# Five of every 120 edge tiles fetched row by row: three by ScalarE, two by SyncE

## The chip, the cores and the metric

The kernel runs on one core of one Trainium2 chip. Time is device microseconds for one execution; lower is better. Five engines work beside one another, each through its own list of instructions in order: TensorE (PE in the profile; its weight loads are PEld), VectorE (DVE), ScalarE (ACT), GpSimd (POOL) and SyncE (SP). POOL, ACT and SP also issue DMA transfers. Engines wait for one another, and for DMA, through semaphores.

## What is computed

A graph layer over 50,000 nodes with 160 features each and 1,650,000 directed edges, sorted by destination. For every edge the source node's row is taken, multiplied by the edge's four attributes, mixed by small weight matrices and summed into the destination; then comes a node-wise product, a ReLU, a residual and a layer norm.

```python
s, v = x[:, :64], x[:, 64:].reshape(n, 32, 3)
ss, vv = s[src], v[src]                    # a gather of 640 bytes for every edge
...
m = concatenate([out0, out1.reshape(-1, 96)], axis=1)
m_agg = segment_sum(m, dst, num_segments=n)
...
x = layernorm(x + x + relu(h))
```

## The kernel before, in words

The kernel sums x[src] times each of four attributes per destination first and applies the weights afterwards, once per node. Edges come in tiles of 128, one edge to a partition. Six tiles make a group, two groups a pair (12 tiles), and ten pairs a segment of 120 tiles. There are 12,522 tiles in 1,044 pairs.

For each pair the work runs so. `gather` (lines 430 to 440) fills one of four `xg` buffers, each of 12 tiles: POOL issues one indirect DMA per tile (line 437), which brings 128 rows of x of 640 bytes each. `spread` (448 to 458) builds on DVE a 0/1 matrix of destinations, `hot` (452), and multiplies it by the attributes, `ha` (455). `group_sums` (475 to 491) multiplies `ha` by the gathered rows on TensorE, two matmul instructions per tile at line 482, into the PSUM tile `ps`. `turn_sums` (493 to 507) transposes `ps` on DVE into `sums` (497) and adds that to a ring of destination sums (506). Each time a block of nodes is complete, `do_block` multiplies its ring columns by the weights (801), and `norm1`, `norm2`, `norm3` finish the rows. `norm2` is one square root on ScalarE (196), placed in ACT's order one pair after the product; `norm3` is on DVE one pair later and waits for it; SyncE sends the result (`do_send`, 899).

The order on SP, PE, DVE and ACT is the order of the Python program (line 979): the loop over pairs at the end writes it out by hand. DVE turns the sums of pair p-1 while PE works on pair p, and then builds `ha` for pair p+1. POOL has its own order: only gathers. It may run ahead until the next `xg` buffer is still being read by PE, which it learns from PE's semaphore.

One tile of 120 is not gathered by POOL. In `list_rows` (376 to 384) DVE clamps its 128 source numbers (`held`, 381) and turns them into byte offsets (`line`, 382). In `rows_by_scalar` (353 to 374) ScalarE loads 32 offsets at a time into registers (365), and then issues one DMA for each row (369, with a register move before it). Each row adds 16 to one of eight semaphores `landed`; Tile's own tracking of these transfers is switched off. The 128 steps are dealt into ACT's order over ten pairs, from the fifth pair of a segment on (lines 1002 to 1009), and the tile is used four pairs after the last (`spots_in`, 351). PE waits in an instruction of its own (481) until 16 x 128 have arrived. The buffers are `xf`, two of them. 102 of the segments have such a set.

SyncE loads the edge data of the next segment (270 and 276), node rows (744, 777), stores the packed edge rows of a table made on the way (718), and sends results (899), all in its written order.

Of the kernel before, what the change touches and what calls it, by code (L numbers as in the profile page):

```python
# [39 lines left out]
F32 = mybir.dt.float32  # L40
I32 = mybir.dt.int32
BF16 = mybir.dt.bfloat16
U8 = mybir.dt.uint8
# [7 lines left out]
P = 128  # L51
# [26 lines left out]
KM = WS - 1  # L78
REST = 15
LEAD = 3  # L80
NF = 1
FB_ = 2
FBEGIN, FWAIT = 4, 4

def plan(n_nodes, n_edges):
# [24 lines left out]
def tile_gnn_resnorm(ctx: ExitStack, tc: tile.TileContext, x, src, dst, attr, W1, W2, W3, W4, W5, Ws, Wv, out, n_edges):  # L110
# [123 lines left out]
    with tc.tile_pool(name="once", bufs=1) as once, tc.tile_pool(name="raw", bufs=2) as rawp, \  # L234
            tc.tile_pool(name="idx", bufs=2) as idxp, tc.tile_pool(name="rows", bufs=4) as rowp, \
            tc.tile_pool(name="hot", bufs=1) as hotp, tc.tile_pool(name="ops", bufs=3) as op, \
            tc.tile_pool(name="sums", bufs=2) as sump, tc.tile_pool(name="ring", bufs=2) as ringp, tc.tile_pool(name="node", bufs=2) as np_, \
            tc.tile_pool(name="ahead", bufs=3) as aheadp, tc.tile_pool(name="outs", bufs=2) as outp, \
            tc.tile_pool(name="psC", bufs=1, space=PSUM) as psC, tc.tile_pool(name="psK", bufs=2, space=PSUM) as psK, \
            tc.tile_pool(name="psP", bufs=1, space=PSUM) as psP, tc.tile_pool(name="psA", bufs=2, space=PSUM) as psA, \  # L240
            tc.tile_pool(name="psM", bufs=2, space=PSUM) as psM, ExitStack() as later_pools:

        spotp, ownp, fetchp, listp, heldp = (
            later_pools.enter_context(tc.tile_pool(name=name, bufs=bufs))
            for name, bufs in (("spot", 3), ("own", 2), ("fetched", FB_), ("list", 2), ("held", 1)))
        extremes = once.tile([P, 2, NSC], F32, name="extremes")
        count_ = once.tile([1, SG], F32, name="count")
        nc.gpsimd.iota(count_, pattern=[[1, SG]], base=0, channel_multiplier=0, allow_small_or_imprecise_dtypes=True)
# [97 lines left out]
                                                        skip_runtime_bounds_check_because="held within bounds")  # L346
            return spot_of.pop(g)

        fetched, fetches, asked, turns = {}, deque(), [], [0]
        landed = [tc.alloc_semaphore(f"landed{i}") for i in range(4 * FB_)]  # L350
        spots_in = [math.ceil((FBEGIN + per * (i + 1) / NF + FWAIT - per) * PG * G) for i in range(NF)]

        def rows_by_scalar(s, i, line, u):

            turn, xf = turns[0], []
            turns[0] += 1
            sem = landed[turn % len(landed)]

            def one(q, e):
                if not q and not e:  # L360
                    xf.append(fetchp.tile([P, D], F32, name="xf"))
                    fetched[s, spots_in[i]] = xf[0], turn
                if not e:
                    r = q * W + u // NK
                    _, asked[:] = nc.values_load_multi_w_load_instructions(
                        line[r:r + 1, i * W:(i + 1) * W], engines=[ET.Activation], min_val=0, max_val=(N - 1) * 4 * D,
                        skip_runtime_bounds_check_because="held within bounds")
                p = q * W + e
                row = nc.scalar.dma_start(xf[0].bitcast(U8)[p:p + 1], xbytes[ds(asked[e], 4 * D)].rearrange("(o f) -> o f", o=1))
                row.then_inc(sem, 16)  # L370
                tc.no_tile_sem_insts.add(row.ins.name)
                tc.add_to_no_dep_group(f"rows{turn}", row.ins)

            fetches.extend(partial(one, q, e) for q in range(P // W) for e in range(W))

        def list_rows(s, u0, ef):

            line = listp.tile([P, NF * W], I32, name="line")
            held = heldp.tile([P, NF, W], F32, name="held")
            for i, at in enumerate(spots_in):  # L380
                nc.vector.tensor_scalar(held[:, i], ef[:, 0, (u0 + at) % NK], 0.0, float(N - 1), op0=ALU.max, op1=ALU.min)
            nc.vector.tensor_scalar(line, held.rearrange("p i e -> p (i e)"), float(4 * D), None, op0=ALU.mult)
            for i, at in enumerate(spots_in):
                rows_by_scalar(s, i, line, u0 + at)

        def place(cast_):

# [42 lines left out]
        def gather(s, placed, u, n):  # L430

            xg = rowp.tile([P, PG * G, D], F32, name="xg")
            rows = [fetched.pop((s, u + j), None) for j in range(n)]
            for j in range(n):
                if rows[j] is None:
                    rows[j] = xg[:, j, :], None
                    nc.gpsimd.indirect_dma_start(  # L437
                        out=xg[:, j, :], out_offset=None, in_=x,
                        in_offset=bass.IndirectOffsetOnAxis(ap=placed[0][:, u + j:u + j + 1], axis=0))
            return rows  # L440
# [34 lines left out]
        def group_sums(p, rows, ha):  # L475

            ps = psA.tile([P, PG, D], F32, name="ps")
            fresh("ps")
            for j, (xr, turn) in enumerate(rows):
                if turn is not None:  # L480
                    nc.tensor.wait_ge(landed[turn % len(landed)], 16 * P * (turn // len(landed) + 1))
                mm = nc.tensor.matmul(ps[:, j // G, :], ha[:, j].rearrange("p k w -> p (k w)"), xr,  # L482
                                      start=j % G == 0, stop=j % G == G - 1)
                if turn is not None:
                    tc.declare_no_dep(mm.ins, group=f"rows{turn}", reason="their own semaphore is waited for")
                    tc.declare_fence(mm.ins, group=f"rows{turn}")
                if j % G == 0:
                    wrote("ps", mm)
                else:
                    written["ps"][-1].append(mm.ins)  # L490
                yield ps
# [485 lines left out]
                after_pair(p + d, f, b)  # L977
        at_last.close()
        later_pools.enter_context(tc.manual_schedule(engines={ET.SP, ET.PE, ET.DVE, ET.Activation}))
        turning, left = None, 0  # L980
        for p, (s, g, ng) in enumerate(pairs):
            if (p + LEAD) % per == 0 and (p + LEAD) // per + 1 < NSC or not p:
                ahead_ = (p + LEAD) // per + 1
                end = reach(ahead_)
                assert end <= 0 or rows_stored[0] == NR or end <= row_start(rows_stored[0])[0][0]
                raws[ahead_] = load(ahead_)
            if p % per == 0 and s + 1 < NSC:
                after_pair(p + 1, do_cast, s + 1)
                after_pair(p + 2, do_place, s + 1)
                if s + 2 == NSC:  # L990
                    after_pair(p + 4, examine_all)
                    after_pair(p + 6, read_flags)
            rows = gather(s, placed[s], (g - s * SG) * G, ng * G)
            for j, ps in enumerate(group_sums(p, rows, has.pop(p))):
                if j == 1 and turning:
                    turn_sums(*turning)
                    turning = None
                if j == 3 and p + 1 < len(pairs):
                    s1, g1, ng1 = pairs[p + 1]
                    has[p + 1] = spread(placed[s1], (g1 - s1 * SG) * G, ng1 * G)  # L1000
                work(1.0)
                if p % per == FBEGIN and not j:
                    assert len(fetches) == (P * NF if 0 < s < NSC - 2 else 0), (p, s, NSC, len(fetches), len(tasks))
                    begun_at, left = p, len(fetches)
                if left:
                    keep = math.floor(P * NF * (1 - (p - begun_at + (j + 1) / (ng * G)) / per))
                    while left > keep:
                        fetches.popleft()()
                        left -= 1
                if packs and p >= START:  # L1010
                    when = p + (j + 1) / (ng * G)
                    todo = math.ceil(len(packs[0]) * min(1, (when - began) / max(1, due[0] - began)))
                    for step in packs[0][done:todo]:
                        if step:
                            step()
                    done = max(done, todo)
                    if done == len(packs[0]):
                        packs.pop(0), due.pop(0)
                        done, began = 0, when
            turning = p, ps  # L1020
            if p == START - 2:
# [12 lines left out]
            hand_over(p)  # L1034
# [162 lines left out]
```

## Time and profile before

| what | us |
|---|---|
| median of the two timed runs | 17926.19 |
| the two runs | 17913.42 and 17938.96 |
| the profiled execution's own time | 18036.58 |
| its span, first to last instruction | 18034.8 |
| POOL busy in the span | 11796.2 |
| DVE busy | 7589.3 |
| PE busy | 7025.2 |
| ACT busy (arithmetic only) | 172.2 |

How to read it: busy time counts work of the engine proper. Register moves and the issuing of DMAs by ACT and SP are not in it, so an ACT that is busy for 1% of the span may still have no time left: its issues stand in the timeline under ACTq, those of SP under SPq. A timeline row gives the start, the time from the first to the end of the last instruction of the row, the engine, the line, the operation, how many are merged, and in brackets the idle time before the first with what ended it. "issue" there means that the profile shows nothing that was waited for; "remote" means a semaphore whose writer the profile could not name.

### The profile page before, as it was taken

To read this page: it belongs to the slowest core of one execution; us is meant where nothing else is said; L and a number is where in the kernel's file an instruction comes from. 1 tells how busy PE (TensorE), PEld (TensorE's weight loads), DVE (VectorE), ACT (ScalarE), POOL (GpSimd) and SP (SyncE) were. 2 spreads that over 40 slices of the span, in tenths; PEclk is the share of its full clock that TensorE was granted. 3 is DMA by queue.
4 is the path that set the end of the run, shared out by engine and by line. 5 is a ranking of instruction groups with operands and counts; after the bars stand their busy time and mean duration, and the time that the engine had idled before them with its cause. 6 is when DMAs were issued, how large, how long until landed. Compare 5 with 4: busy or idle time off the path is not lost.

```text
span 18034.8 us, 122135 instructions
## 1 busy us (share of the span) xinstructions
PE 7025.2 (39%) x28971; PEld 6194.0 (34%) x28972; DVE 7589.3 (42%) x12430; ACT 172.2 (1%) x273; POOL 11796.2 (65%) x12433
## 2 busy tenths in 40 slices
PE   3343343334433333333334334333333433333333
PEld 3233333333333333333333333333333333333333
DVE  7344245334524443453345245434533453454233
ACT  0000000000000000000000000000000000000000
POOL 6566666666666666666666666666666666666666
PEclk6666666666666666666666666666666566666666
DMA  2222222222222222222222222222232222222222
GB/s 72 74 72 80 75 73 70 83 75 73 72 82 74 72 81 75 72 70 84 74 73 78 80 70 72 80 74 73 69 86 74 72 74 79 71 73 72 74 70 65
DMA packets 866482, 1343.45 MB, mean 74 GB/s; under 512 B 270014, under 2 KB 637602, under 8 KB 863094
## 3 DMA queue, kind: packets, MB, share of 16 engines
q0 software_dynamic: 596160, 1018.24, 21.5%
q1 hardware_dynamic: 242218, 308.07, 5.3%
q10 hardware_dynamic: 27376, 9.29, 0.3%
q8 instruction: 231, 3.78, 0.1%
q14 instruction: 497, 4.07, 0.1%
HBM read 1263.28 MB, written 71.42 MB: 74 GB/s over the span
## 4 chain that ended last, share of the span: by engine, by line
POOL 33%; issue 32%; PE 13%; another core or an unknown queue 11%; DVE 4%; DMA 3%; DVEq 0%; ACTq 0%; SPq 0%; POOLq 0%; ACT 0%
POOL xg L437 33%; PE ps L482 12%; DMA xg<-in_x,si 3%; PE phb L801 2%; DVE ha L455 1%; DVE ring L506 0%; DVE hot L452 0%; DVE prow L667 0%; DVE pra L667 0%; DVE sums L497 0%; DVE ring L792 0%; DVE pri L662 0%; DVE marks L660 0%; DVE xr L788 0%
## 5 line engine op out<-in xcount | busy, mean ns | idle before, releaser
L437 POOL DMA_INDIRECT xg<-in_x,si x12420 | 11792.7, 949 | 6203.6 <-issue 3640.9
L482 PE MATMUL ps<-xg,ha 128*128 128x160 f32 x24840 | 6390.0, 397 | 9847.6 <-issue 8559.2
L482 PEld LDWEIGHTS ps<-xg,ha 128*128 128x128 f32 x24840 | 5423.2, 267 | 10659.3 <-issue 9304.4
L497 DVE STREAM_TRANSPOSE sums<-ps 128x320 f32<-128x320 f32 x1044 | 530.6, 508 | 8243.2 <-remote 5581.5
L455 DVE TENSOR_TENSOR ha<-hot,pk 128x1536 f32<-128x1536 f32 x1044 | 1830.0, 1753 | 53.8 <-DVE hot L452 12.9
L801 PE MATMUL phb<-BWk,ring 128*128 128x160 f32 (+1 forms) x3910 | 1217.7, 394 | 791.8 <-issue 791.0
L801 PEld LDWEIGHTS phb<-BWk,ring 128*128 128x128 f32 (+1 forms) x3910 | 950.0, 271 | 782.4 <-issue 781.9
L506 DVE TENSOR_TENSOR ring<-ring,sums 128x160 f32 x2087 | 682.2, 327 | 312.5 <-issue 203.7
L186 DVE SCALAR_TENSOR_TENSOR y<-phb,xt 128x320 f32<-128x320 f32 x196 | 95.1, 485 | 1315.9 <-remote 638.9
L452 DVE TENSOR_TENSOR hot<-bank,rel 128x384 f32<-128x384 f32 x1044 | 572.8, 549 | 76.2 <-DMA xt<-in_x 73.2
L667 DVE COPY_PREDICATED prow<-marks,prow 128x2370 f32<-128x2370 int32 (+5 forms) x198 | 549.7, 2776 | 1.1
L792 DVE STREAM_TRANSPOSE ring<-xr 128x1280 f32<-128x1280 f32 x188 | 465.2, 2474 | 7.1 <-DVE xr L788 0.6
L667 DVE COPY_PREDICATED pra<-marks,pra 128x1580 f32<-128x1580 int32 (+5 forms) x198 | 378.0, 1909 | 0.0
L788 DVE TENSOR_TENSOR xr<-xr,bank 128x1280 f32<-128x1280 f32 x188 | 278.9, 1483 | 18.2 <-DVE bank L787 6.4
L196 ACT ACTIVATE rstd<-mv,eps_t 128x2 f32<-128x2 f32 x196 | 58.0, 296 | 16430.7 <-DVE mv L191 9545.5
L482 PE MATMUL ps<-xf,ha 128*128 128x160 f32 x204 | 71.0, 439 | 289.9 <-DVE ha L455 127.6
L482 PEld LDWEIGHTS ps<-xf,ha 128*128 128x128 f32 x204 | 42.8, 256 | 316.6 <-issue 237.9
L503 DVE TENSOR_TENSOR ring<-ring 128x196 f32<-128x196 f32 (+20 forms) x485 | 149.2, 372 | 1.8
L202 DVE TENSOR_SCALAR o<-y,mv,rstd 128x160 f32<-128x160 f32 x391 | 131.5, 377 | 26.9 <-issue 11.1
L664 DVE COPY_PREDICATED_SCALAR hit<-marks,none 128x395 int32 (+5 forms) x198 | 130.0, 656 | 10.1 <-DVE pri L662 3.3
L751 DVE MEMSET ring<- 128x1280 f32 (+1 forms) x98 | 119.3, 1218 | 22.7 <-issue 22.7
L190 DVE BATCH_NORM_STATS2 st<-y 128x6 f32<-128x160 f32 x391 | 121.6, 311 | 6.7
(351 smaller groups left out, 2048.0 us busy)
## 6 DMA issues: line engine op xcount, KB each, us to landing
xf<-in_x ACTq DMA_DIRECT2D x13056, 0.6 KB
xg<-in_x,si POOLq DMA_INDIRECT x12420
xr<-in_x SPq DMA_DIRECT2D x187, 640.0 KB
r<-edges SPq DMA_DIRECT2D x100, 384.0 KB
edges<-prow SPq DMA_DIRECT2D x1330, 27.8 KB
xt<-in_x SPq DMA_DIRECT2D x195, 160.0 KB
out<-o SPq DMA_DIRECT2D x195, 160.0 KB
pra<-in_attr SPq DMA_DIRECT2D x10, 2370.0 KB
```

Source lines behind the costliest of these rows:

```text
L202: nc.vector.tensor_scalar(o[:n, i], y[:n, i], mv[:n, i, 0:1], rstd[:n, i:i + 1], op0=ALU.subtract, op1=ALU.mult)
L437: nc.gpsimd.indirect_dma_start(out=xg[:, j, :], out_offset=None, in_=x, in_offset=bass.IndirectOffsetOnAxis(ap=placed[0][:, u + j:u + j + ...
L452: idle[:] = [nc.vector.tensor_tensor(hot[:, :n], slotsP[:, 0:W].unsqueeze(1).to_broadcast([P, n, W]), rel[:, u:u + n].unsqueeze(2).to_broa ...
L455: nc.vector.tensor_tensor(ha[:, :n], hot[:, :n].unsqueeze(2).to_broadcast([P, n, NK, W]), pk[:, :, u:u + n].rearrange("p k u -> p u k").un ...
L482: mm = nc.tensor.matmul(ps[:, j // G, :], ha[:, j].rearrange("p k w -> p (k w)"), xr, start=j % G == 0, stop=j % G == G - 1)
L497: nc.vector.transpose(at[:, :ng], ps[:, :ng].rearrange("p g (b f) -> p g b f", f=FB))
L503: nc.vector.tensor_tensor(ring[k][:, b, :past], ring[k][:, b, :past], ring[k - 1][:, b, S:S + past], op=ALU.add)
L506: nc.vector.tensor_tensor(here, here, at[:, i], op=ALU.add)
L667: nc.vector.copy_predicated(what[:n, a:e], mi[:, r].unsqueeze(2).to_broadcast([n, e - a, what.shape[2]]), what[:n, a + d:e + d])
L788: nc.vector.tensor_tensor(xr[:, :nq], xr[:, :nq], sumP[:, :nq].unsqueeze(2).to_broadcast([P, nq, D]), op=ALU.mult)
L792: nc.vector.transpose(ring[k][:, :, c0:c0 + nq * W].rearrange("p b (w q) -> p q b w", q=nq), xr[:, :nq].rearrange("p q (b f) -> p q b f", ...
L801: wrote("misc", nc.tensor.matmul(ph[:nb], ring[k][:, i, c0:c0 + nb], BWk[:, i, :], start=i == 0, stop=i == ND - 1))
```

## The change

ScalarE now fetches three tiles of 120 and SyncE two, each row by row, so POOL gathers 115 tiles of 120 in place of 119. A class `Fetcher` holds an engine, its tile pool, its places in the segment and its own set of semaphores. ScalarE has four tiles (pool `scalar`, tiles named `xscalar`) and 16 semaphores, SyncE three (`sync`, `xsync`) and 12. The places are tiles 18, 58 and 98 for ScalarE and 44 and 104 for SyncE; before, the one place was tile 96. Each engine's rows are dealt into its order evenly over the same ten pairs. `held` and `line` hold five sets of numbers in place of one. PE's wait for the rows is part of the matmul (`wait_op`) and no longer an instruction ahead of it. To make room, `sums` has one buffer in place of two. Which edges are summed where is unchanged.

```diff
-NF = 1
-FB_ = 2
+BY_SCALAR, BY_SYNC = 3, 2
...
-            tc.tile_pool(name="sums", bufs=2) as sump, ...
+            tc.tile_pool(name="sums", bufs=1) as sump, ...
...
+        class Fetcher:
+            def __init__(self, engine, et, pool, n, place):
...
+                self.landed = [tc.alloc_semaphore(f"{pool.name}{i}") for i in range(4 * (n + 1))]
+                self.spots = [math.ceil((FBEGIN + per * (i + 1) / n + FWAIT - per) * PG * G) + place for i in range(n)]
...
+                def one(q, e):
...
+                    if not e:
+                        r = q * W + u // NK
+                        _, self.asked = nc.values_load_multi_w_load_instructions(
+                            line[r:r + 1, :], engines=[self.et], min_val=0, max_val=(N - 1) * 4 * D, ...)
+                    p = q * W + e
+                    row = self.engine.dma_start(tile_[0].bitcast(U8)[p:p + 1],
+                                                xbytes[ds(self.asked[e], 4 * D)].rearrange("(o f) -> o f", o=1))
+                    row.then_inc(sem, 16)
...
+            def deal(self, gone):
+                keep = math.floor(P * self.n * (1 - gone))
+                while self.left > keep:
+                    self.rows.popleft()()
+                    self.left -= 1
+        fetchers = [Fetcher(*f) for f in ((nc.scalar, ET.Activation, scalarp, BY_SCALAR, 2), (nc.sync, ET.SP, syncp, BY_SYNC, 8)) if f[3]]
...
-                if turn is not None:
-                    nc.tensor.wait_ge(landed[turn % len(landed)], 16 * P * (turn // len(landed) + 1))
                 mm = nc.tensor.matmul(...)
+                if key:
+                    mm.wait_op(sem, count, "sem-ge")
...
+                for f in fetchers:
+                    if f.left:
+                        f.deal((p - begun_at + (j + 1) / (ng * G)) / per)
```

More of the change, by code (lines that the diff above doesn't have):

```diff
@@ L236, in tile_gnn_resnorm @@
             tc.tile_pool(name="hot", bufs=1) as hotp, tc.tile_pool(name="ops", bufs=3) as op, \
-            tc.tile_pool(name="sums", bufs=2) as sump, tc.tile_pool(name="ring", bufs=2) as ringp, tc.tile_pool(name="node", bufs=2) as np_, \
+            tc.tile_pool(name="sums", bufs=1) as sump, tc.tile_pool(name="ring", bufs=2) as ringp, tc.tile_pool(name="node", bufs=2) as np_, \
             tc.tile_pool(name="ahead", bufs=3) as aheadp, tc.tile_pool(name="outs", bufs=2) as outp, \
@@ L241, in tile_gnn_resnorm @@
             tc.tile_pool(name="psM", bufs=2, space=PSUM) as psM, ExitStack() as later_pools:
-        spotp, ownp, fetchp, listp, heldp = (
+        spotp, ownp, listp, heldp, scalarp, syncp = (
             later_pools.enter_context(tc.tile_pool(name=name, bufs=bufs))
-            for name, bufs in (("spot", 3), ("own", 2), ("fetched", FB_), ("list", 2), ("held", 1)))
+            for name, bufs in (("spot", 3), ("own", 2), ("list", 2), ("held", 1),
+                               ("scalar", BY_SCALAR + 1), ("sync", BY_SYNC + 1)))
         extremes = once.tile([P, 2, NSC], F32, name="extremes")
@@ L347, in find @@
             return spot_of.pop(g)
[L349 to L374, printed above, removed]
@@ new lines, in tile_gnn_resnorm, with prepare, begin @@
+        fetched = {}
+        class Fetcher:
+            def __init__(self, engine, et, pool, n, place):
+                self.engine, self.et, self.pool, self.n = engine, et, pool, n
+                self.rows, self.turn, self.left, self.asked = deque(), 0, 0, []
+                self.landed = [tc.alloc_semaphore(f"{pool.name}{i}") for i in range(4 * (n + 1))]
+                self.spots = [math.ceil((FBEGIN + per * (i + 1) / n + FWAIT - per) * PG * G) + place for i in range(n)]
+                assert all(0 <= at < per * PG * G for at in self.spots)
+            def prepare(self, s, line, at, u):
+                turn, tile_ = self.turn, []
+                self.turn += 1
+                sem, count = self.landed[turn % len(self.landed)], 16 * P * (turn // len(self.landed) + 1)
+                def one(q, e):
+                    if not q and not e:
+                        tile_.append(self.pool.tile([P, D], F32, name="x" + self.pool.name))
+                        fetched[s, at] = tile_[0], sem, count, f"{self.pool.name}{turn}"
+                    if not e:
+                        r = q * W + u // NK
+                        _, self.asked = nc.values_load_multi_w_load_instructions(
+                            line[r:r + 1, :], engines=[self.et], min_val=0, max_val=(N - 1) * 4 * D,
+                            skip_runtime_bounds_check_because="held within bounds")
+                    p = q * W + e
+                    row = self.engine.dma_start(tile_[0].bitcast(U8)[p:p + 1],
+                                                xbytes[ds(self.asked[e], 4 * D)].rearrange("(o f) -> o f", o=1))
+                    row.then_inc(sem, 16)
+                    tc.no_tile_sem_insts.add(row.ins.name)
+                    tc.add_to_no_dep_group(f"{self.pool.name}{turn}", row.ins)
+                self.rows.extend(partial(one, q, e) for q in range(P // W) for e in range(W))
+            def begin(self, wanted):
+                assert len(self.rows) == wanted * self.n * P
+                self.left = len(self.rows)
+            def deal(self, gone):
[3 more added lines that the diff above has]
+                    self.left -= 1
@@ L376, in list_rows @@
+        fetchers = [Fetcher(*f) for f in ((nc.scalar, ET.Activation, scalarp, BY_SCALAR, 2), (nc.sync, ET.SP, syncp, BY_SYNC, 8)) if f[3]]
+        wanted = [(f, at) for f in fetchers for at in f.spots]
+        assert len({at for _, at in wanted}) == len(wanted)
         def list_rows(s, u0, ef):
-            line = listp.tile([P, NF * W], I32, name="line")
-            held = heldp.tile([P, NF, W], F32, name="held")
-            for i, at in enumerate(spots_in):
+            line = listp.tile([P, len(wanted), W], I32, name="line")
+            held = heldp.tile([P, len(wanted), W], F32, name="held")
+            for i, (f, at) in enumerate(wanted):
@@ L381, in list_rows @@
                 nc.vector.tensor_scalar(held[:, i], ef[:, 0, (u0 + at) % NK], 0.0, float(N - 1), op0=ALU.max, op1=ALU.min)
-            nc.vector.tensor_scalar(line, held.rearrange("p i e -> p (i e)"), float(4 * D), None, op0=ALU.mult)
-            for i, at in enumerate(spots_in):
-                rows_by_scalar(s, i, line, u0 + at)
+            nc.vector.tensor_scalar(line, held, float(4 * D), None, op0=ALU.mult)
+            for i, (f, at) in enumerate(wanted):
+                f.prepare(s, line[:, i], at, u0 + at)
@@ L435, in gather @@
                 if rows[j] is None:
-                    rows[j] = xg[:, j, :], None
+                    rows[j] = xg[:, j, :], None, None, None
                     nc.gpsimd.indirect_dma_start(
@@ L478, in group_sums @@
             fresh("ps")
-            for j, (xr, turn) in enumerate(rows):
-                if turn is not None:
-                    nc.tensor.wait_ge(landed[turn % len(landed)], 16 * P * (turn // len(landed) + 1))
+            for j, (xr, sem, count, key) in enumerate(rows):
                 mm = nc.tensor.matmul(ps[:, j // G, :], ha[:, j].rearrange("p k w -> p (k w)"), xr,
                                       start=j % G == 0, stop=j % G == G - 1)
-                if turn is not None:
-                    tc.declare_no_dep(mm.ins, group=f"rows{turn}", reason="their own semaphore is waited for")
-                    tc.declare_fence(mm.ins, group=f"rows{turn}")
+                if key:
+                    mm.wait_op(sem, count, "sem-ge")
+                    tc.declare_no_dep(mm.ins, group=key, reason="their own semaphore is waited for")
+                    tc.declare_fence(mm.ins, group=key)
                 if j % G == 0:
@@ L979, in tile_gnn_resnorm @@
         later_pools.enter_context(tc.manual_schedule(engines={ET.SP, ET.PE, ET.DVE, ET.Activation}))
-        turning, left = None, 0
+        turning = None
         for p, (s, g, ng) in enumerate(pairs):
@@ L1002, in tile_gnn_resnorm @@
                 if p % per == FBEGIN and not j:
[L1003 to L1009, printed above, removed]
+                    begun_at = p
+                    for f in fetchers:
+                        f.begin(0 < s < NSC - 2)
+                for f in fetchers:
+                    if f.left:
+                        f.deal((p - begun_at + (j + 1) / (ng * G)) / per)
                 if packs and p >= START:
```

## The prediction

> **What bounds the kernel now.** I read the page's busy times and costliest groups first, then the timeline of POOL over one stretch, then DVE, PE and ACT over the same stretch. From the page:
>
> ```profile
> span 18034.8 us, 122135 instructions
> L437 POOL DMA_INDIRECT xg<-in_x,si x12420 | 11792.7, 949 | 6203.6 <-issue 3640.9
> xf<-in_x ACTq DMA_DIRECT2D x13056, 0.6 KB
> ```
>
> No engine is full: POOL is busy for 11,793 us of 18,035. POOL's timeline shows how its time goes:
>
> ```profile
> 8936.52 0.95 POOL L437 DMA_INDIRECT xg<-in_x,si  x1 [4.73 <-PE ps L482]
> ...
> 8972.60 0.95 POOL L437 DMA_INDIRECT xg<-in_x,si  x1 [6.34 <-issue]
> 8973.85 0.94 POOL L437 DMA_INDIRECT xg<-in_x,si  x1 [0.31 <-issue]
> ...
> 9000.16 0.95 POOL L437 DMA_INDIRECT xg<-in_x,si  x1 [0.30 <-issue]
> 9005.43 0.94 POOL L437 DMA_INDIRECT xg<-in_x,si  x1 [4.32 <-remote]
> ```
>
> From 8972.60 to 9000.16 are 23 gathers, 22 steps in 27.56 us: 1.253 us a tile, of which 0.30 us is a gap that the profile ascribes to nothing. Then POOL stands for 4.3 us at a pair's border. Pure issue would be 12,420 x 1.253 = 15,562 us; the missing 2,470 us are such stands. They are there before ScalarE fetches its first row (at 292 us, below):
>
> ```profile
> 133.40 0.95 POOL L437 DMA_INDIRECT xg<-in_x,si  x1 [4.27 <-PE ps L482]
> 167.77 0.95 POOL L437 DMA_INDIRECT xg<-in_x,si  x1 [4.59 <-PE ps L482]
> 200.51 0.95 POOL L437 DMA_INDIRECT xg<-in_x,si  x1 [3.00 <-remote]
> 219.19 0.95 POOL L437 DMA_INDIRECT xg<-in_x,si  x1 [3.98 <-remote]
> ```
>
> So 24 tiles take 34.4 us (133.40 to 167.77), and a run of 12 takes 18.7 us (200.51 to 219.19). What does POOL stand for? For PE's word that a buffer is free. DVE waits for PE too, and is let go in the same moment:
>
> ```profile
> 8989.65 0.60 DVE L665 COPY_PREDICATED hit<-marks,pri 128x395 int32<-128x395 int32 x1
> 9005.19 0.52 DVE L497 STREAM_TRANSPOSE sums<-ps 128x320 f32<-128x320 f32 x1 [14.94 <-remote]
> ```
>
> While POOL issues, something holds the other engines up. The view of busy times in two neighbouring stretches of 17 us shows it on PE (the count in brackets is instructions):
>
> ```profile
> 8936.00:8953.00 17.00, 13.07 (x50) 12.38 (x50) 15.39 (x37) 0.30 (x1) 12.52 (x14) 0.63 0.22 59
> 8953.00:8970.00 17.00, 2.72 (x7) 1.62 (x6) 2.58 (x8) 0.00 (x0) 10.21 (x11) 0.57 0.35 87
> ```
>
> The first stretch begins as POOL resumes after a stand (8936.52 above): 50 matmuls, 50 weight loads, 37 DVE instructions. In the second, POOL still issuing, there are 7, 6 and 8. I call the two kinds quick and held stretches. ACT, which only issues rows there, shows the same thing:
>
> ```profile
> 8970.67 8.16 ACTq L369 DMA_DIRECT2D xf<-in_x  x26
> 8955.20 14.03 ACTq L369 DMA_DIRECT2D xf<-in_x  x6
> ```
>
> Quick: 8.16 / 26 = 0.314 us a row. Held: five steps in 14.03 us, 2.81 us a row. Four lists of 32 rows in which no other wait stands:
>
> ```profile
> 9042.90 48.62 ACTq L369 DMA_DIRECT2D xf<-in_x  x32
> 9093.97 32.57 ACTq L369 DMA_DIRECT2D xf<-in_x  x32
> 9136.42 28.75 ACTq L369 DMA_DIRECT2D xf<-in_x  x32
> 9167.63 30.36 ACTq L369 DMA_DIRECT2D xf<-in_x  x32
> ```
>
> and the register loads ahead of each list, with the first and last row of all sets:
>
> ```profile
> L365 ACTq TENSOR_LOAD <-line x408: 4/2202/3080, 289.7 to 17854.5; - x136
> L369 ACTq DMA_DIRECT2D xf<-in_x x13056: 2/228/1667, 292.1 to 17889.7; - x198
> ```
>
> A set costs ACT 140.3 + 4 x 2.2 = 149.1 us. A period of 120 tiles is (17,889.7 - 292.1) / 102 = 172.5 us. One set thus takes 86% of ACT's time. POOL sets the pace today, and ACT, at 1% busy on the page, has little left.
>
> **The change part by part.** All is reckoned per period of 172.5 us, of which 102 change.
>
> POOL: four gathers fewer, 115 in place of 119. If POOL kept the pace, the period would be 172.5 x 115/119 = 166.7 us, 5.8 us less.
>
> ACT: 384 rows and 12 register loads in place of 128 and 4. At the present mean pace that is 3 x 149.1 = 447 us; if every row were quick, 384 x 0.314 + 12 x 2.2 = 147 us. These are the two ends, and 166.7 lies between, near the low one. To choose I split a cycle of 24 tiles. Without other waits 34.4 / 149.1 x 128 = 29.5 rows fit, with 0.92 loads (2.0 us). With q us quick, (q - 2.0) / 0.314 + (34.4 - q) / 2.81 = 29.5 gives q = 8.4 us, and 26.0 us held. In the changed kernel 24 POOL tiles are 1/4.79 of a period and bring 80.1 rows and 2.5 loads. The held 26.0 us take 9.3 rows; the other 70.8 need 22.2 us and the loads 5.5 us. The cycle is 26.0 + 27.7 = 53.7 us, and the period 257 us: ACT becomes the bound, and POOL, out of buffers, stands until the rows land. If POOL runs 12 tiles at a time (18.7 us, 8.4 quick and 10.3 held), each such run carries 40.1 rows and 1.25 loads: 3.7 rows held, 36.4 x 0.314 + 2.75 = 14.2 us quick, 24.5 us, and a period of 235 us. Both runs stand in the trace, so I take the middle, 246 us. The held share does shrink as POOL stands longer; the sum has that already, since only POOL's own running time is held.
>
> Behind ACT's rows is queued the square root of each finished block (196), on which DVE waits for norm3 before it can turn the next sums. A late ACT therefore stops DVE, and with it PE, and the four pairs of slack ahead of the tile's use do not help.
>
> SP: 256 rows and 8 loads. SP's own single stores show its price in a held stretch; these ten starts lie 18.61 us apart:
>
> ```profile
> 3610.10 0.23 SPq L718 DMA_DIRECT2D selves<-mine  x1
> ...
> 3628.71 0.00 SPq L718 DMA_DIRECT2D selves<-mine  x1
> ```
>
> That is 2.1 us each. In a period of 246 us with about 112 held, SP sends 40 to 53 rows held and the rest in some 68 us of the 134 quick, plus 17.6 us of loads. It fits beside ACT, so I cost it at nothing; if that cover is gone it is the third rival. Queued behind SP's rows are the next segment's edge loads (270) and the results.
>
> DVE: four more `held` and a `line` of 160 in place of 32 numbers:
>
> ```profile
> L382 DVE TENSOR_SCALAR line<-held x102: 180/181/334, 289.5 to 17718.0; 128x32 int32<-128x32 f32 x102
> L381 DVE TENSOR_SCALAR held<-r x99: 167/180/378, 881.1 to 17717.8; 128x32 f32<-128x32 f32 x99
> ```
>
> 4 x 0.18 us and at most as much again, 1 us a period, hidden by DVE's waits for PE (14.94 us at one place above); uncovered it is 0.1 ms in all. `sums` with one buffer: written and read by DVE alone, in order, nothing. PE's wait inside the matmul: nothing while rows are early; when late, PE stands either way. DMA traffic: rows of 640 bytes move from one queue to another; nothing.
>
> Sum: 102 x (246 - 172.5) = 7,497 us on the profiled 18,036.58 us is 25,534 us. The median of the timed runs is 110 us under the profiled execution; less that, 25,424, so 25,400 us.
>
> [...]
>
> **The rivals.**
>
> First, the other side: ACT keeps up, and POOL's four gathers are saved. Its mechanism: held stretches need POOL's unbroken run, and an ACT that is a little late breaks that run, so that most rows go at the quick price. For it speaks the 147 us that ACT needs at 0.314 us, below 166.7. Against it speaks that POOL's present stands of 4.3 us in 34.4 leave only 8.4 us quick. It decides at (166.7 - 26.4) / 384 = 0.365 us a row; today's mean is 140.3 / 128 = 1.10. Its time: 17,926 - 102 x 5.8 = 17,334 us. The same would come about if the held stretches were not there in the timed runs; the profiled execution is only 0.6% longer than they, and POOL's stands, which fill that time, come with the held stretches, so I think they are.
>
> [...]
>
> Second, no difference: ACT keeps up, but 512 more rows a period lengthen POOL's stands by the 5.8 us saved, 0.011 us a row. Against it: with no rows beside them 24 tiles took 34.37 us (133.40 to 167.77), 1.432 each, and with ScalarE's rows beside them 23 took 32.83 us (8972.60 to 9005.43), 1.427 each; a row costs POOL nothing that shows. 17,926 us.
>
> Third, slower still: SP is the bound. Its results wait for DVE in order:
>
> ```profile
> SPq L899 <- DVE o L202: 3050.4, 46, 120.2
> ```
>
> 66 us each, with rows queued behind. Two in a period, wholly in quick time: 112 + 68 + 17.6 + 132 = 330 us, 17,926 + 102 x 157 = 34,000 us. Against it: rows dealt in the written order come after the wait as much as before it, and SP has three buffers.
>
> **How the numbers follow.** ACT as the bound 0.63; SP 0.05; ACT keeping up 0.27; no difference 0.05. The likeliest case has its own range: from 223 us a period (runs of 12, held rows at half their price: 7.4 rows held, 13.0 us quick) to 264 us (runs of 38 tiles, a third of a period: 44 us held with 15.7 rows, 44.1 us quick), that is 23,000 to 27,300 us. To hold 8 in 10 the range must reach the first rival: 17,300 to 27,500 us. About 2% is what a measurement of this kernel can tell from no change: faster 0.27, same 0.05, slower 0.68.
>
> **What would show it.** Right: ACT's rows stand back to back through every period, POOL's stands at pair borders grow from 4.3 us to tens, PE or DVE wait for ACT's square root or the `xscalar` rows, periods of 223 to 264 us. Wrong: ACT's lists of 32 take 10 to 14 us each and POOL's stands stay near 4.3 us; then the held price does not carry over. If SP's queue is the one without gaps, the third rival holds.

## The result and the profile after

| | us |
|---|---|
| before, median of two runs | 17926.19 |
| changed kernel, median of two runs | 26170.57 (26057.72 and 26283.42) |
| ratio, 95% interval | 1.4598 (1.449 to 1.4707) |
| profiled execution of the changed kernel | 26057.72 |

The changed kernel is slower by 46%; 25,400 us were predicted. Chips differ for this kernel: the kernel before took 18,090 us on the chip of the first experiments and 15,590 us on those of the second and third, so every comparison below is made with the run of before on the same chip.

From the page of the changed kernel (busy us and mean ns after the bar, then the idle time before and its main releaser):

```profile
span 26056.0 us, 228216 instructions
L459 POOL DMA_INDIRECT xg<-in_x,si x12012 | 11406.5, 950 | 14611.5 <-PE ps L502 9920.8
L199 DVE RECIPROCAL rstd<-rstd 128x2 f32<-128x2 f32 x196 | 32.1, 164 | 12511.7 <-ACT rstd L195 12427.6
```

POOL issues 408 gathers fewer in 11,406 us, each still 0.95 us, but is now idle for 14,612 us in place of 6,204 (some 3,600 to 3,700 us of each are the gaps of 0.30 us between gathers). The longest of the waits (us in total, times, longest):

```profile
DVE rstd L199 <- ACT rstd L195: 12427.6, 170, 105.5
POOL xg L459 <- PE ps L502: 9920.8, 416, 71.9
...
PE ps L502 <- DMA xscalar<-in_x: 747.1, 33, 41.7
```

DVE waits for ScalarE's square root 170 times, 73 us each; POOL then waits for PE 416 times, 24 us each. PE itself hardly waits for the rows. Why the square root is late is seen in ACT's timeline:

```profile
9000.72 120.82 ACTq L376 DMA_DIRECT2D xscalar<-in_x  x183
9121.59 0.29 ACT L195 ACTIVATE rstd<-mv,eps_t 128x2 f32<-128x2 f32 x1 [145.91 <-issue]
9124.24 120.45 ACTq L376 DMA_DIRECT2D xscalar<-in_x  x192
9244.74 0.29 ACT L195 ACTIVATE rstd<-mv,eps_t 128x2 f32<-128x2 f32 x1 [122.85 <-issue]
```

Between these two square roots lie 192 rows back to back with their register loads, and nothing else: 120.45 us. Held and quick stretches are still there. POOL and ACT around one border, the two views one behind the other:

```profile
9015.39 0.95 POOL L459 DMA_INDIRECT xg<-in_x,si  x1 [0.30 <-issue]
9020.96 0.95 POOL L459 DMA_INDIRECT xg<-in_x,si  x1 [4.61 <-remote]
```

```profile
9003.53 16.11 ACTq L376 DMA_DIRECT2D xscalar<-in_x  x7
```

```profile
9020.35 16.87 ACTq L376 DMA_DIRECT2D xscalar<-in_x  x23
```

Seven rows in 16 us up to POOL's stand, 23 in the 17 us from about its end on (with a register load among them). The view of the row DMAs by line gives the period (minimum, median and maximum ns, then first and last start):

```profile
L376 ACTq MOVE xscalar<-in_x x39168: 1/29/1659, 290.5 to 25979.1; - x200
L376 ACTq DMA_DIRECT2D xscalar<-in_x x39168: 1/228/1537, 290.5 to 25979.2; - x200
```

(25,979.2 - 290.5) / 102 = 251.9 us; 246 was predicted.

### The profile page after: what moved, and what is told of

Same layout as the page of the kernel before. It is cut to its first block, busy times and chain, and to the rows that moved or that the text cites. A ratio compares the mean times of both kernels' runs of the same rounds, so it can differ in the third digit from the quotient of the medians.

```text
span 26056.0 us, 228216 instructions
## 1 busy us (share of the span) xinstructions
PE 6105.7 (23%) x28971; PEld 5708.7 (22%) x28972; DVE 7617.5 (29%) x12838; ACT 171.8 (1%) x273; POOL 11410.0 (44%) x12025
## 3 DMA queue, kind: packets, MB, share of 16 engines
q0 software_dynamic: 576576, 984.79, 14.4%
## 5 line engine op out<-in xcount | busy, mean ns | idle before, releaser
L459 POOL DMA_INDIRECT xg<-in_x,si x12012 | 11406.5, 950 | 14611.5 <-PE ps L502 9920.8
L502 PE MATMUL ps<-xg,ha 128*128 128x160 f32 x24024 | 5455.5, 377 | 18145.8 <-issue 17477.2
L502 PEld LDWEIGHTS ps<-xg,ha 128*128 128x128 f32 x24024 | 4821.9, 253 | 18500.4 <-issue 17815.5
L502 PE MATMUL ps<-xscalar,ha 128*128 128x160 f32 x612 | 185.9, 390 | 1092.9 <-DMA xscalar<-in_x 747.1
L502 PEld LDWEIGHTS ps<-xscalar,ha 128*128 128x128 f32 x612 | 132.9, 251 | 1120.4 <-DMA xscalar<-in_x 785.8
L502 PE MATMUL ps<-xsync,ha 128*128 128x160 f32 x408 | 114.5, 368 | 416.3 <-DMA xsync<-in_x 386.3
L502 PEld LDWEIGHTS ps<-xsync,ha 128*128 128x128 f32 x408 | 86.1, 243 | 425.9 <-DMA xsync<-in_x 391.2
```

The source lines that it names most:

```text
L459: nc.gpsimd.indirect_dma_start(out=xg[:, j, :], out_offset=None, in_=x, in_offset=bass.IndirectOffsetOnAxis(ap=placed[0][:, u + j:u + j + ...
```

## The experiments

The theory: while POOL issues gathers back to back, the instructions of the other engines are held up; ScalarE's queue, with 384 rows a period, then is the bound, and the square root behind its rows hands its lateness on to DVE, PE and POOL. The rivals: the two queues share one limit or SyncE is the bound; rows are dear in themselves or by the gathers' traffic; the order, not the amount, is at fault; the small parts of the change cost something.

### First chip: which queue, and what makes a row dear

Four kernels, one run each, beside one run of the kernel before, 18,090.03 us there. The changed kernel itself was not run in this group.

**ScalarE's three sets alone.**

```diff
-BY_SCALAR, BY_SYNC = 3, 2
+BY_SCALAR, BY_SYNC = 3, 0
```

> Three sets by ScalarE, none by SyncE. Theory (ScalarE's queue alone is the bound, at the prices of the prediction): 117 gathers in a period are 4.875 runs of 24, each with 78.8 rows and 2.46 register loads; the held 26.0 us take 9.3 rows, the other 69.5 need 21.8 us and the loads 5.4 us, a cycle of 53.2 us and a period of 259 us; with runs of 12 some 236 us; with the 251.9 us measured as the scale about 248. So 25,000 to 26,300 us, nearly all of the loss still there. Rival (the rows of both queues share one limit: 640 rows in the measured period of 251.9 us are 0.394 us a row): 384 rows take 151 us, less than POOL's 117/119 of 172.5 us, so about 17,700 us. Rival (SyncE's queue is the bound): also about 17,700 us.

Measured: 25,692.6 us. From this run's view of waits, and its row DMAs by line:

```profile
DVE rstd L199 <- ACT rstd L195: 12524.0, 170, 107.7
```

```profile
L376 ACTq DMA_DIRECT2D xscalar<-in_x x39168: 1/228/1507, 290.3 to 25613.0; - x200
```

The same wait, as long as in the full change, and a period of (25,613.0 - 290.3) / 102 = 248.3 us. ScalarE's part alone makes the loss; one limit for the rows of both queues, which would have given 17,700 us, is excluded.

**SyncE's two sets beside the old one of ScalarE** (`BY_SCALAR, BY_SYNC = 1, 2`).

> One set by ScalarE as in the kernel before, two by SyncE. Theory (each queue has a limit of its own, and a row costs SyncE what it costs ScalarE): ScalarE needs 149 us, not the bound; SyncE has 52.5 rows and 1.64 loads to a run of 24 gathers, which is a cycle of 26.0 + 13.6 + 3.6 = 43.2 us, a period of 211 us (187 with runs of 12): 19,400 to 21,900 us. If SyncE's rows are hidden, as the prediction has them, 17,500 us. Rival (one limit for the rows of both queues, 0.394 us a row): 384 rows in 151 us, POOL bounds, 17,500 us. In the profile: SyncE's rows back to back and DVE not waiting for the square root (theory), or gaps between SyncE's rows (hidden).

Measured: 24,899.19 us, more than the theory's 21,900. From its view of waits, and the row DMAs by line:

```profile
POOL xg L459 <- PE ps L502: 8407.2, 345, 108.7
DVE sa L807 <- DMA sa<-selves: 7642.3, 187, 121.8
...
PE ps L502 <- DMA xsync<-in_x: 4657.3, 122, 119.6
```

```profile
L376 SPq DMA_DIRECT2D xsync<-in_x x26112: 1/228/5024, 290.0 to 24817.2; - x200
```

The square root is out of the list. DVE now waits for node rows (`sa`) that SyncE asks for behind its fetched rows, and PE for the rows themselves. SyncE's period is (24,817.2 - 290.0) / 102 = 240.5 us. So SyncE is a bound of its own, only 3% below ScalarE's 248.3: taking away either engine's extra rows gives back little, because the other's stay.

**One gather a pair.**

```diff
+            one = rows.index(None)
             for j in range(n):
                 if rows[j] is None:
-                    rows[j] = xg[:, j, :], None, None, None
+                    rows[j] = xg[:, one, :], None, None, None
+                    if j != one:
+                        continue
```

> Three sets and two as in the changed kernel, but POOL gathers only one tile of each pair and TensorE uses it for all that POOL would have gathered: eleven of twelve gathers are left out. Theory (rows are dear only while POOL issues gathers back to back): ScalarE's rows go at 0.314 us, 384 x 0.314 + 12 x 2.2 = 147 us, and SyncE's 256 x 0.314 + 17.6 = 98 us; the period is 147 to 165 us and the whole 15,500 to 17,000 us. Rival (the rows are dear in themselves, or the two queues contend with each other): the period stays above 220 us, over 23,000 us.

Measured: 16,679.66 us. ACT's timeline and row DMAs:

```profile
9049.06 79.17 ACTq L376 DMA_DIRECT2D xscalar<-in_x  x192
9128.27 0.29 ACT L195 ACTIVATE rstd<-mv,eps_t 128x2 f32<-128x2 f32 x1 [78.99 <-issue]
```

```profile
L376 ACTq MOVE xscalar<-in_x x39168: 29/29/38, 214.6 to 16613.7; - x200
L376 ACTq DMA_DIRECT2D xscalar<-in_x x39168: 227/228/1082, 214.6 to 16613.8; - x200
```

192 rows take 79 us in place of 120, although both engines issue all their rows: the rows are not dear in themselves, nor do the two queues alone hold each other up. None of ACT's register moves takes longer than 38 ns; in the changed kernel the longest took 1,659. The longest of SyncE's is 510 ns here, 1,470 there. The period is 160.8 us, and ScalarE still has no gap: even with next to no gathers beside them the three sets leave the kernel only 8% faster than before.

**Short gathers.** Each of POOL's gathers brings 16 bytes of a row in place of 640, from other addresses, and TensorE repeats these four numbers forty times. The count of gathers stays at 12,012.

```diff
-                    rows[j] = xg[:, j, :], None, None, None
+                    rows[j] = xg[:, j, 0:4].unsqueeze(1).to_broadcast([P, D // 4, 4]), None, None, None
...
-                        out=xg[:, j, :], out_offset=None, in_=x,
+                        out=xg[:, j, 0:4], out_offset=None, in_=x.rearrange("n (a f) -> (n a) f", f=4),
```

> [...] Theory (what holds the rows up is that POOL issues gathers back to back, not the bytes they move): time and period stay within 3% of the changed kernel's, 25,300 to 26,900 us, if POOL's step of 1.25 us a tile stays. Rival (the transfers of the gathers crowd the DMA engines, and rows wait for their share of them): ScalarE's rows go at the quick price and the period falls to 147 to 167 us, 15,500 to 17,400 us.

Measured: 26,392.33 us. Its row on the page, and the wait for the square root:

```profile
L459 POOL DMA_INDIRECT xg<-in_x,si x12012 | 11387.7, 948 | 14962.1 <-PE ps L502 10104.3
```

```profile
DVE rstd L199 <- ACT rstd L195: 12752.3, 172, 107.5
```

With one fortieth of the bytes a gather takes POOL the same 0.95 us and nothing else moves much either: 1.459 times the kernel before here, 1.460 for the changed kernel beside its own. What holds the rows up is the gathers, not the bytes that they carry. Their queue has 384,384 packets on this run's page and 576,576 on the changed kernel's, 32 a gather in place of 48: the packets fell by a third only, so issuing the gathers and working off their packets are not told apart.

### Second chip: the split, taken down

Here the kernel before took 15,590.17 us (13 runs). The four expectations were written with the prices of the first chip.

**The new code with the old split** (`BY_SCALAR, BY_SYNC = 1, 0`).

> The changed kernel's code with the split of the kernel before: one set by ScalarE, none by SyncE. What is left of the change is one buffer fewer for the sums, the wait inside the matmul, and other tiles and semaphores. Theory (these cost nothing, the whole loss is in the queues that issue the rows): the time of the kernel before within 1%, 17,750 to 18,100 us. Rival (the wait inside the matmul or the single buffer of the sums holds TensorE or VectorE up): 18,300 us or more.

Measured: 15,589.62 us, ratio 1.000 (0.999 to 1.0009). The sums' single buffer and the wait in the matmul cost nothing on this chip. Both kernels take 14% less than the kernel before took on the first chip, and the page and POOL's timeline of this run say where:

```profile
span 15588.9 us, 122136 instructions
L459 POOL DMA_INDIRECT xg<-in_x,si x12420 | 11773.0, 948 | 3792.4 <-issue 3544.7
```

```profile
8999.52 0.95 POOL L459 DMA_INDIRECT xg<-in_x,si  x1 [0.30 <-issue]
...
9069.73 0.95 POOL L459 DMA_INDIRECT xg<-in_x,si  x1 [0.30 <-issue]
```

In these 70 us POOL never stands; between gathers lie gaps of 0.30 us, one of 0.42. 12,420 x 1.25 = 15,525 us is the whole time. The busy times of the same two stretches of 17 us in which the prediction shows 50 and 7 matmuls:

```profile
8936.00:8953.00 17.00, 12.43 (x30) 7.14 (x29) 7.02 (x13) 0.00 (x0) 12.76 (x14) 0.50 0.35 87
8953.00:8970.00 17.00, 12.97 (x38) 8.54 (x38) 11.56 (x11) 0.00 (x0) 13.02 (x14) 0.60 0.28 69
```

POOL issues 14 gathers in each, and PE does 30 and 38 matmuls. ACT's register moves say the same of the whole run:

```profile
L376 ACTq MOVE xscalar<-in_x x13056: 29/29/37, 244.0 to 15374.3; - x198
```

None took longer than 37 ns. With one set by ScalarE and the same number of gathers as the kernel before, there are no held stretches here.

**One and one** (`1, 1`).

> One set by ScalarE, one by SyncE: 118 gathers a period. Theory (SyncE has a limit of its own, as the run with one set and two showed): in the kernel before SyncE waits some 98 us of a period for results; a set at the mixed price is 149 us, so 51 us are missing, about 46 rows, which must go in quick time while POOL stands, 46 x 0.314 = 15 us more: a period near 187 us and 19,400 us (18,300 to 20,000). Rival (one set still fits beside SyncE's stores, POOL sets the pace): 172.5 x 118/119 = 171 us, 17,780 us, slightly better than both kernels.

Measured: 15,497.38 us, ratio 0.994 (0.9923 to 0.9957). POOL's pace times 118/119 would be 0.9916.

**Two and none** (`2, 0`).

> Two sets by ScalarE, none by SyncE. Theory (ScalarE's queue is the bound as soon as its rows do not fit; the prediction's split of quick and held stretches): 118 gathers are 4.92 runs of 24, each with 52.1 rows and 1.63 loads; 9.3 rows held in 26.0 us, 42.8 in 13.4 us, loads 3.6 us: a cycle of 43.0 us, a period of 212 us; with runs of 12, 187 us; the middle 199 us, 20,600 us (19,400 to 22,000). Rival (ScalarE slows only beyond two sets, or gives way): 17,700 us.

Measured: 15,478.08 us, one run, 0.7% less than before. The theories of both runs missed, and the rivals, by which POOL keeps the pace, held: without held stretches a second set fits on either engine. The theory's prices under held stretches stay untested at two sets by ScalarE.

**No square root behind the rows** (all five sets).

```diff
-        nc.scalar.activation(rstd[:n, :m], mv[:n, :m, 1], AF.Sqrt, bias=eps_t[:n])
+        nc.vector.tensor_scalar(rstd[:n, :m], mv[:n, :m, 1], EPS * HALF * HALF, None, op0=ALU.add)
```

> Three sets and two, but the square root of the norm is left out of ScalarE's queue: VectorE adds the small constant instead and takes the reciprocal, so the square root itself is left out of the computation. Theory (it is the throughput of ScalarE's queue that bounds; the square root behind the rows is only where the lateness shows): the time stays, 25,000 to 26,500 us, VectorE's wait for ScalarE at the reciprocal is gone, and TensorE waits for the xscalar rows or VectorE for SyncE's loads in its place. Rival (the order is the cause: rows could run late in their four pairs of slack if nothing stood behind them): more than 2,000 us are saved, below 24,000 us.

Measured: 17,013.63 us. Without the full change on this chip it could not be read, so both were run together on a third.

### Third chip: the change, its best part, and a pause

Before: 15,593.70 us (7 runs).

**The changed kernel again.**

> The changed kernel once more, since the kernel before took 18,090 us on the chip of the first experiments, in which POOL's runs have held stretches, and 15,590 us on that of the second, whose traces show none (POOL's steps 1.25 us with three stands over 1 us). Theory (ScalarE's queue bounds in either case): without held stretches a row costs 0.283 us and a register move 0.063 us, 384 x 0.346 + 12 x 2.35 = 161 us against POOL's 115 x 1.247 = 143 us; with what else stands in that queue the 163.9 us a period of the run without the square root, 16,900 to 17,300 us, some 9% slower than before there. With held stretches 25,900 to 26,400 us, 45% slower. Rival (without held stretches the change gains what POOL is spared): 15,080 us.

Measured: 17,249.21 us, ratio 1.1068 (1.1043 to 1.1094). ACT's timeline, its moves, and the wait for its square root:

```profile
9015.11 0.30 ACT L195 ACTIVATE rstd<-mv,eps_t 128x2 f32<-128x2 f32 x1 [96.83 <-issue]
9015.18 79.48 ACTq L376 DMA_DIRECT2D xscalar<-in_x  x192
9094.71 0.30 ACT L195 ACTIVATE rstd<-mv,eps_t 128x2 f32<-128x2 f32 x1 [79.30 <-issue]
9094.78 78.17 ACTq L376 DMA_DIRECT2D xscalar<-in_x  x192
```

```profile
L376 ACTq MOVE xscalar<-in_x x39168: 29/29/38, 244.0 to 17135.8; - x200
L376 ACTq DMA_DIRECT2D xscalar<-in_x x39168: 227/228/1213, 244.1 to 17135.9; - x200
```

```profile
DVE rstd L199 <- ACT rstd L195: 5073.3, 151, 61.0
```

The change loses on this chip too, by the same mechanism at the quick price: the rows stand back to back, 384 of them and 12 loads take (17,135.9 - 244.1) / 102 = 165.6 us, where POOL would need 115 x 1.25 = 144.

**No square root, again.**

> Again the kernel without the square root on ScalarE (it is left out of the computation), now beside the changed kernel on the same chip. Theory (throughput of the queue): within 3% of the changed kernel, with or without held stretches. Rival (order: the square root behind the rows is the cause): over 5% faster than the changed kernel.

Measured: 17,025.38 us, 1.3% under the changed kernel. Its waits:

```profile
DVE sa L807 <- DMA sa<-selves: 1789.8, 86, 104.9
PE ps L502 <- DMA xscalar<-in_x: 1737.9, 101, 40.6
```

PE now waits for `xscalar`, 1,738 us against 206 in the run above. The wait has moved from behind the queue to the rows themselves. The amount of rows is the cause, and the square root is only where it shows. This is shown for a chip without held stretches only, by one run.

**Two and one** (`2, 1`).

> Two sets by ScalarE, one by SyncE: 117 gathers a period. Theory without held stretches: ScalarE needs 2 x (128 x 0.346 + 4 x 2.35) = 107 us, SyncE's one set took 38 us a period of its waits (9,478 to 3,201 us in all is 62 us), both fit in 148 us, and POOL sets the pace: 148.3 x 117/119 = 145.8 us, 15,340 us, 1.6% faster than before: a version better than both kernels. With held stretches ScalarE's two sets bound: 187 to 212 us a period, 19,400 to 22,000 us, slower than before. Rival: SyncE's queue fills, and it is slower than before without held stretches too.

Measured: 15,445.92 us, ratio 0.9905 (0.9889 to 0.9922): faster than both kernels on this chip, by 0.95% and not the 1.6% expected. SyncE's wait for a result, here and below it in the run with the old split:

```profile
SPq L920 <- DVE o L201: 2634.0, 112, 69.0
```

```profile
SPq L920 <- DVE o L201: 10483.2, 175, 94.3
```

SyncE still has time left: by these two lines its one set took (10,483.2 - 2,634.0) / 102 = 77 us a period of this wait, more than either figure of the expectation, 38 and 62, and still fits. POOL's steps of 1.3 us and over, counted in the trace, add 136 us over 1.25 each, against 35 with the old split: 100 of the 250 us that two gathers a period save go into stands, two of them of 19 and 33 us. Where the kernel before has held stretches this split was not run.

**A memset behind each gather** (all five sets).

```diff
+                    nc.gpsimd.memset(pause, 0.0)
```

> Three sets and two as in the changed kernel, with a memset of one number a partition on POOL behind each gather, which adds some 0.1 to 0.4 us to a step. Theory (held stretches come of a backlog: 12 tiles more lengthen a cycle from 18.7 to 34.4 us, 1.31 us a tile against POOL's step of 1.253, so that POOL runs ahead by 0.06 us a tile of something that drains, and a step over 1.31 us leaves none): with held stretches in the kernel before, they vanish here, ScalarE's rows go at 0.35 us, and the time falls from 26,100 to 17,000 to 19,000 us. Rival (the others are held for as long as POOL issues, at whatever pace): 25,500 us or more. Where the kernel before has no held stretches this tells nothing on them: 17,000 to 19,000 us by either, by POOL's step.

A memset of this size takes POOL 97 ns in the changed kernel (L122, `eps_t`); with a gap of 0.30 us more it is 0.4 us.

Measured: 18,940.34 us, on a chip without held stretches, so it tells nothing on them. It would not have anywhere, for the memsets are not where they were meant to be. The view of their line, and POOL's timeline:

```profile
L463 POOL MEMSET pause<- x12012: 88/99/832, 1.7 to 2431.8; 128x1 f32 x197
```

```profile
1169.15 0.95 POOL L460 DMA_INDIRECT xg<-in_x,si  x1 [0.30 <-issue]
1170.10 1261.84 POOL L463 MEMSET pause<- 128x1 f32 x8067
2432.58 0.94 POOL L460 DMA_INDIRECT xg<-in_x,si  x1 [0.64 <-issue]
```

All 12,012 memsets have run by 2,432 us of 18,939, and 8,067 of them stand in one row between two gathers. The order on POOL is not written out by hand as on the other four engines, and the memsets came ahead of the gathers that they were to follow. From 2,432 us on every gather follows the last with no memset between them. The loss beside the changed kernel, 1,691 us, is mostly that one row: PE waits 1,263 us for the gather behind it. Only 81 memsets lie singly between two gathers, in the first 118 us; there, but for four, each fits into the gap of 0.30 us, and the step stays 1.25. Whether a slower POOL ends the held stretches is open.

## Why the prediction was right

**The bound.** ScalarE's queue, back to back in every period, as forecast (the 0.63 case). 25,400 against 26,170.57, 771 us too low: the period of 251.85 in place of 246 is 597 us, about 73 fewer fell outside the periods, and the median, which I put 110 under the profiled execution, lay 113 over it; rounding down took 24.

**The split into quick and held.** Counted in the trace of the changed kernel, with a step of a row DMA or its register move called held from 0.6 us on:

| per period | forecast (middle of the two runs) | counted |
|---|---|---|
| held | 112 us, 40 rows, 2.81 us each | 120 us, 56 rows, 2.14 us each |
| quick | 108 us, 344 rows, 0.314 us each | 106 us, 328 rows, 0.324 us each |
| 12 register loads | 26.4 us | 24.9 us |
| sum | 246 us | 251 us |

The method held; the held row was taken too dear, from one list of six, and held time a little short, and these partly cancel. That the number came within 3% is therefore in part luck, and so is the middle of 235 and 257 us, for which the prediction had no other ground than that both runs stand in the trace.

What the prediction took for one price comes in steps. PE in the stretch from which the 2.81 us were read, in the kernel before:

```profile
8960.86 0.42 PE L482 MATMUL ps<-xg,ha 128*128 128x160 f32 x1 [2.40 <-issue]
8963.66 0.43 PE L482 MATMUL ps<-xg,ha 128*128 128x160 f32 x1 [2.38 <-issue]
8966.47 0.43 PE L482 MATMUL ps<-xg,ha 128*128 128x160 f32 x1 [2.38 <-issue]
8969.26 0.42 PE L482 MATMUL ps<-xg,ha 128*128 128x160 f32 x1 [2.37 <-DMA xg<-in_x,si]
```

A weight load and a matmul take 2.80 us here, as long as a row's move and its DMA. In the trace their starts alternate, one every 0.70 us: ACT's DMA at 8960.14, PE's matmul at 8960.86, ACT's move at 8961.53, the weight load at 8962.26, and so on. Counted over the whole trace, 37% of ACT's held steps are of 0.70 us and 54% of 1.40 (each within 0.1) in the kernel before, 47% and 48% in the changed one. A held row, two steps, so costs mostly 1.40 to 2.80 us; the list of six stood at the dear end, and 2.14 is the mean in the changed kernel. Why the short step is more frequent in the changed kernel was not tested.

**The path to the end.** The square root stops DVE, then PE, then POOL, and the four pairs of slack do not help: 12,428 us against 747 for the rows themselves. POOL's waits for PE have grown to 24 us on average, from the stands of 4.3. The waits and ACT's timeline show this path.

**SyncE at nothing.** Right for the sum, since 240.5 lies under 251.9, but its working was wrong, and with a chance of 0.05 for SyncE as the bound I was near a mistake. The step "40 to 53 rows held and the rest in some 68 us of the 134 quick, plus 17.6 us of loads" left out what else SyncE issues. In the run with two sets by SyncE its 256 rows took 190 us a period, the loads 16, its stores of packed edges 21 and the rest 12 (counted in the trace); waiting for results took only 2. In the changed kernel itself these waits came to 20 us of a period. The stores were on the page I had read. Their price was read a little low too: the line that the prediction shows at 3628.71 is the ninth start, eight steps and so 2.33 us each; the tenth, 0.01 us behind it, is a quick one already.

**What cost nothing.** DVE's four more `held`, the sums' single buffer and the wait in the matmul: ratio 1.000 with the old split on a chip without held stretches, so the last two cost nothing there. DVE's part is not in that run; it is 0.1 ms at most by the prediction's rows, and was not measured by itself.

**The first rival, ACT keeps up.** It fell even where its condition, no held stretches, was met. Its point of decision, 0.365 us a row, was worked out against POOL's 166.7 us, a pace that includes POOL's stands. Those stands go with the held stretches: POOL then takes 144 us, and the point falls to (144 - 28) / 384 = 0.30 us (28 for 12 loads of some 2.3), under the 0.34 that a row and its move cost there: 78.17 us for 192 rows and six loads with a median of 2.27 us. Two conditions that occur only together have to be put into a rival together. Moving gathers from POOL to the other queues gained little even without held stretches, 0.9905 with two sets and one, and three and two lost, 1.1068.

## What to carry to other kernels

An engine at 1% busy may be full: add up what its queue issues, stores and loads included, before you give it more, for each engine that is to take part of the work. Read the price of an issue in the stretches where it will be issued; the spread of the register moves (29/29/38 ns or 1/29/1659) tells at a glance whether they are held up. When a rival takes away a condition, take away all that the trace shows to come with it, and time small gains on more than one chip. When you add an instruction to an engine whose order you do not write yourself, look in the trace where it went.

## What the runs showed of the hardware

Held stretches belong to some chips or occasions and not to others: the kernel before took 17,926 and 18,090 us with them, 15,590 and 15,594 without, at a granted clock of 0.62 with and 0.57 without, so a higher clock is not the reason. While held, single instructions are late, and not only those that issue transfers: register moves took up to 1.66 us in place of 0.03, and 91 to 95% of ACT's held steps were of 0.70 or 1.40 us. The bytes of the gathers are not the cause (26,392 us with a fortieth of them); with a twelfth of the gathers ACT had no late move (16,680 us, none over 38 ns, one of SyncE's 510), but many gathers are not enough, since the second chip ran 14 in 17 us with no move of ACT over 37 ns. What else it takes, and what the engines share in these steps, stays open: no run here varied it, nor tells whether the recording of the instructions has a part in it.
